# One field by 512 samples a chunk: the field groups folded into the top net's first layer, pooled sums kept in PSUM, 206 and 195 tiles fetched by SyncE and ScalarE

## The chip, the core and the metric

The kernel runs on one core of a Trainium2 chip. The metric is the time of one execution in microseconds of the device; of the kernel before there are three runs, with a median of 16514.44 us (16500.01 to 16524.78). The profile is of one further execution. Its engines are named as in its page: PE (TensorE matmul), PEld (its weight loads), DVE (VectorE), ACT (ScalarE), POOL (GpSimd), SP (SyncE).

## The reference

A click model for 16384 samples. Each sample has F = 69 indices and a label index into a table of 100001 rows of E = 96 floats. With u the rows of the indices and ql the row of the label:

```python
q = jnp.broadcast_to(ql[:, None, :], u.shape)
z = jnp.concatenate([q, u, q - u, q * u], axis=-1)
h = _dice(z @ W1 + b1, a1, EPS_DICE)           # 384 -> 64
h = h @ W2 + b2                                # 64 -> 16
att = h @ W3 + b3                              # 16 -> 1
pre = jnp.where(eff, u * att, 0.0)             # eff: index < 100000
pooled = jnp.einsum('gf,bfe->bge', window, pre).reshape(u.shape[0], G * E)
x = jnp.concatenate([pooled, ql], axis=-1)     # G = 10 groups of fields, and ql: 11 * 96
h = _dice(_bn_eval(x @ Wf1 + bf1, EPS_BN), af1, EPS_DICE)    # 1056 -> 200
h = _dice(_bn_eval(h @ Wf2 + bf2, EPS_BN), af2, EPS_DICE)    # 200 -> 80
return h @ Wf3 + bf3                           # 80 -> 1
```

`_dice(x, a)` is `(a * (1 - p) + p) * x` with p the sigmoid of x scaled. `window` is a 10 by 69 matrix of zeros and ones that says which fields a group sums. All is in float32.

## The kernel before, in words

The samples are worked in 32 blocks of 512. A block's 512 x 69 rows are cut into 69 chunks of 512 rows, and two chunks make a pair: 1104 pairs in all. 64 of a block's chunks hold 8 samples by 64 fields ("main"), the other five hold one of the last five fields for all 512 samples ("tail"). A chunk is four tiles of 128 rows.

*Fetching.* A tile is gathered by one indirect DMA on POOL (`gather`, L266). 369 of the 8832 tiles are fetched otherwise: 199 by SyncE and 170 by ScalarE, row by row with a DMA of 384 bytes each (`Singles.fetch`, L301) after loads of 32 offsets each into registers (L286). They land in `ring`, a separate buffer of 8 + 4 tiles, and PE waits for them by semaphore. SyncE starts a tile every 5.5 pairs. ScalarE issues 20 rows in every pair (`ACT_ROWS`), in its own program order between its activations. POOL also gathers 128 tiles of label rows. It writes `u`, of which `upool` has 15 buffers of a pair each.

*A pair.* The order is written out by hand: `at(step, work)` fills a plan, and the pair's step runs its pieces in the order given; each engine does its part of them in that order.

- `fetch` (L359): PE transposes the four tiles of each chunk (L325) into PSUM `ptr` (two buffers), DVE copies it to `uT` (L376) and multiplies it by the label's rows to `quT` (L379, L386).
- `hidden` (L388): PE makes `ph` of `uT` and `quT` (L399 to L403), both chunks side by side in 64 columns of the array each; ACT makes the sigmoid (L405) and a scale and shift of it (L406), DVE the product `y` (L407). The label's share of the first layer comes in through 32 further rows: a main chunk's `uT` has a one-hot pattern in them, and the weights `A` hold the label's products, made per block by `head_rows` (L342).
- Attention of main chunks: every fourth pair, `attend_rows` (L409) makes the products `prow` (L414), which ACT copies (L416); `spread` (L428) transposes them back (L431), and DVE multiplies with the window to `rw` (L436). `pool` (L448), seven pairs behind its fetch, multiplies the gathered tiles by `rw` on PE (16 rows of the profile per pair, `acc`, L325) and DVE copies the sums of the ten groups to `pooled` (L470). So a `u` buffer is held until its `pool`.
- Attention of tail chunks: `attend_tail` makes `pa` (L423) and DVE `pre = (pa + b) * uT` (L424).
- The top net of a block (`top1` to `top3`, L489 to L522), once per block, is spread over ten later pairs: 16 products a half (10 groups, the label, five tail fields) into `p` (L502), then activations, `p2` (L513) and `p3` (L521).

Near the end (`CLOSE` = 8 pairs) the order changes, and the last block's top net is done in four quarters of 128 samples.

PE writes a float32 matmul as two passes, which the profile counts singly (a transpose as one).

Of the kernel before, what the change touches and what calls it, by code (L numbers as in the profile page):

```python
# [11 lines left out]
F32 = mybir.dt.float32  # L12
# [15 lines left out]
FM = 64  # L28
NTAIL = F - FM
NS = BLK // FM  # L30
NMAIN = BLK // NS
NCH = NMAIN + NTAIL
NQ = BLK // P
NT = NCH * 4
NCOL = NT + NQ
NPAIR = NBLK * NCH // 2
# [4 lines left out]
POOL_LAG = 7  # L41

NIDS = 4

EARLY = 20

CLOSE = 8
# [15 lines left out]
def chunk_of(c):  # L63

    n, k = divmod(c, NCH)
    if n == NBLK - 1 and k >= EARLY:
        k = NMAIN + k - EARLY if k < EARLY + NTAIL else k - NTAIL
    return n, k


class Pack:
# [28 lines left out]
    wtile=(0, P, 2 * G),  # L100
)
FAR = Pack(
    wrow=(0, E, NTAIL * G),
    Wf1=(0, E, (G + 1) * D1),
# [6 lines left out]
    bf3=(0, P, 1),  # L111
)
# [3 lines left out]
def rec_kernel(  # L116
# [8 lines left out]
    far: bass.AP,  # L125
    out: bass.AP,
# [7 lines left out]
    upool = ctx.enter_context(tc.tile_pool(name="upool", bufs=15))  # L134
    tpool = ctx.enter_context(tc.tile_pool(name="tpool", bufs=4))
    ypool = ctx.enter_context(tc.tile_pool(name="ypool", bufs=6))
    rpool = ctx.enter_context(tc.tile_pool(name="rpool", bufs=2))
# [3 lines left out]
    def by_field(ap):  # L141

        return ap.rearrange("e (s o) -> e s o", o=1).to_broadcast([ap.shape[0], NS, FM])

# [19 lines left out]
    nc.sync.dma_start(out=wf, in_=far)  # L164

# [8 lines left out]
    Wp = w1[:, 3, :]  # L174


    As = [const.tile([P, NMAIN // 4, H1], F32, name=f"A{i}") for i in range(2)]
    nc.vector.tensor_sub(As[0][0:E, 0, :], w1[:, 1, :], w1[:, 2, :])
    nc.vector.tensor_copy(As[0][0:E, 1:, :], As[0][0:E, 0:1, :].to_broadcast([E, NMAIN // 4 - 1, H1]))
    nc.vector.tensor_copy(As[1][0:E], As[0][0:E])  # L180
    A = As[0][0:E, 0, :]
    uTs = [[const.tile([P, 512], F32, name=f"uT{v}_{i}") for i in range(3)] for v in range(4)]

    def ones():
        for i in range(3):
            for v in range(4):
                nc.vector.tensor_copy(
                    uTs[v][i][E:P, :].rearrange("e (s f) -> e s f", f=FM),
                    by_field(ident[E:P, E + v * NS : E + (v + 1) * NS]),
                )  # L190
# [17 lines left out]
    v2 = const.tile([P, 32], F32, name="v2")  # L208
    nc.vector.memset(v2, 0.0)
# [4 lines left out]
    R = NEAR.of(wn, "wtile")  # L214
    wr = FAR.of(wf, "wrow").rearrange("e (f g) -> e f g", g=G)


    wf1 = FAR.of(wf, "Wf1").rearrange("e (k n) -> e k n", n=D1)
# [20 lines left out]
    with tc.tile_pool(name="prep_ps", bufs=1, space=PSUM) as pps:  # L239
        pv = pps.tile([P, E], F32, name="pv")  # L240
        nc.tensor.matmul(pv, NEAR.of(wn, "W2T"), w3b, start=True, stop=True)
        nc.vector.tensor_copy(vrep, pv)
        for i in range(2):
            nc.vector.tensor_copy(v2[i * H1 : (i + 1) * H1, i : i + 1], pv[i * H1 : (i + 1) * H1, 0:1])
# [7 lines left out]
    ps_acc = ctx.enter_context(tc.tile_pool(name="ps_acc", bufs=1, space=PSUM))  # L252
    ps_m = ctx.enter_context(tc.tile_pool(name="ps_m", bufs=1, space=PSUM))


    V = const.tile([E, NTAIL, D1], F32, name="V")

    def tail_weights(f):
        nc.vector.tensor_scalar_mul(V[:, f, :], wf1[:, 0, :], wr[:, f, 0:1])
        for g in range(1, G):  # L260
            nc.vector.scalar_tensor_tensor(
                V[:, f, :], wf1[:, g, :], wr[:, f, g : g + 1], V[:, f, :], ALU.mult, ALU.add
            )

    def gather(table, dst, index):
# [5 lines left out]
        )  # L271

# [69 lines left out]
    def head_rows(n):  # L342

        for h in range(2):
            pc = ps_x.tile([P, NMAIN // 8, H1], F32, tag="x", name=f"pc{n}_{h}")
            for k in range(NMAIN // 8):
                x = (h * NMAIN // 8 + k) * 4 * NS
                nc.tensor.matmul(pc[E:P, k, :], qTs[n % 2][:, x : x + 4 * NS], Cq, start=True, stop=True)
            nc.scalar.copy(As[n % 2][E:P, h * NMAIN // 8 : (h + 1) * NMAIN // 8, :], pc[E:P])

    turns = [0] * 4

    def room(k):

        v = k % 4 if k < NMAIN else turns.index(min(turns))
        turns[v] += 1
        return uTs[v][turns[v] % len(uTs[v])]

    def fetch(i, between=None):  # L359

        u = upool.tile([P, 8, E], F32, tag="u", name=f"u{i}")
        uT = []
        quT = tpool.tile([E, 2, 512], F32, tag="quT", name=f"quT{i}")
        for j in range(2):
            if j == 1 and between:
                between()
            n, k = chunk_of(2 * i + j)
            ptr = ps_tr.tile([E, 512], F32, tag="tr", name=f"ptr{i}_{j}")
            for t in range(4):
                if single(2 * i + j, t):  # L370
                    wait_for_single(2 * i + j, t)
                else:
                    gather(rows, u[:, 4 * j + t, :], ids[n][:, 4 * k + t : 4 * k + t + 1])
                read_rows(nc.tensor.transpose, ptr[:, t * P : (t + 1) * P], u, 2 * i + j, t, ident)
            uT.append(room(k))
            nc.vector.tensor_copy(uT[j][0:E], ptr)  # L376
            q = qTs[n % 2][0:E]
            if k < NMAIN:
                nc.vector.tensor_tensor(  # L379
                    quT[:, j, :].rearrange("e (s f) -> e s f", f=FM),  # L380
                    ptr.rearrange("e (s f) -> e s f", f=FM),
                    by_field(q[:, k * NS : (k + 1) * NS]),
                    ALU.mult,
                )
            else:
                nc.vector.tensor_tensor(quT[:, j, :], ptr, q[:, 0:BLK], ALU.mult)  # L386
        return u, uT, quT

    def hidden(i, uT, quT):

        ph = ps_h.tile([P, 512], F32, tag="h", name=f"ph{i}")
        places = [chunk_of(2 * i + j) for j in range(2)]
        sums = [ph[j * H1 : (j + 1) * H1, :] for j in range(2)]
        for (n, k), p in zip(places, sums):
            if k >= NMAIN:
                nc.tensor.matmul(p, Cq, qTs[n % 2], start=True, stop=False)  # L396
        for j, ((n, k), p) in enumerate(zip(places, sums)):
            if k < NMAIN:
                nc.tensor.matmul(p, As[n % 2][:, k // 4, :], uT[j], start=True, stop=False)  # L399
            else:  # L400
                nc.tensor.matmul(p, A, uT[j][0:E], start=False, stop=False)  # L401
        for j, p in enumerate(sums):
            nc.tensor.matmul(p, Wp, quT[:, j, :], start=False, stop=True)  # L403
        y = ypool.tile([P, 512], F32, tag="y", name=f"y{i}")
# [349 lines left out]
```

## Time and profile before

| | |
|---|---|
| runs | 16514.44, 16500.01, 16524.78 us |
| the profiled execution: span from its first to its last instruction | 10780.4 us |
| its mean granted TensorE clock | 0.749 |
| what lies around the span, to the median of the runs | 5734.0 us, of which the trace shows nothing |
| instructions | 204439 |
| moved by DMA | 460.70 MB, 43 GB/s on average |
| gathers on POOL | 8463 + 128 |
| rows issued by SyncE, ScalarE | 25472, 21760 |
| pairs of chunks | 1104 |

For the profiled execution there is no time beside its span; the runs in the first row were made without a profile.

How to read the page: in its list of groups, a line gives the source line, the engine, the operation, what is written and read, the count, the busy time in us with the mean of one in ns, and the idle time of the engine before it with what ended most of it. In a timeline, each row is the start in us, the duration in us, the engine and what it does, with the number of instructions merged; an engine's name with a q is its sequencer, which issues DMAs and waits. In a view of one source line, each row has the least, median and largest duration in ns and the first and last start. In the waits, a row gives who waited for whom, the total in us, how often, and the longest.

### The profile page before, as it was taken

Reading aid. Unit: us, or ns where it says so; the run is one execution under the profiler, and the core shown is the slowest. Engines: PE = TensorE matmul, PEld = TensorE weight load, DVE = VectorE, ACT = ScalarE, POOL = GpSimd, SP = SyncE. Lnnn points to the kernel's source line nnn. Section 1 sums busy time; section 2 is a strip of 40 time slices with the busy share of each in tenths; the row PEclk is TensorE's granted clock in tenths of the full one; section 3 lists DMA queues with packets and bytes.
Section 4 is the critical chain, followed back from the end, with each engine's and each line's share of the span. In section 5 each row is a group of like instructions: output and inputs, shape, how many; then the busy total and the mean of one; then the engine's idle time right before and its main releaser. Section 6 shows DMA issues by size and latency. Waiting matters only on the chain.

```text
span 10780.4 us, 204439 instructions
## 1 busy us (share of the span) xinstructions
PE 8756.9 (81%) x41797; PEld 4310.8 (40%) x41797; DVE 4235.1 (39%) x7535; ACT 1884.4 (17%) x2761; POOL 8110.8 (75%) x8597
## 2 busy tenths in 40 slices
PE   6888888888887788877888788888887887888888
PEld 3434444434433344433433344333343343443335
DVE  4333333333333333333333343333333334333333
ACT  1111111111111111111111111111111111111112
POOL 7777777777777777777777777777777777777776
PEclk7777777677777777777777777777777777777778
DMA  2222222222222222222222222222222222222221
GB/s 50 42 42 42 45 42 42 42 42 45 42 42 42 45 42 42 42 42 45 42 42 42 42 44 42 42 42 42 44 42 42 42 42 44 42 42 42 42 42 34
DMA packets 372495, 460.70 MB, mean 43 GB/s; under 512 B 232114, under 2 KB 232626, under 8 KB 371106
## 3 DMA queue, kind: packets, MB, share of 16 engines
q0 software_dynamic: 274912, 422.81, 18.9%
q1 hardware_dynamic: 52802, 16.36, 1.0%
q10 hardware_dynamic: 43520, 8.44, 0.7%
q14 instruction: 925, 7.58, 0.2%
q8 instruction: 336, 5.51, 0.2%
HBM read 446.81 MB, written 0.07 MB: 41 GB/s over the span
## 4 chain that ended last, share of the span: by engine, by line
POOL 40%; PE 21%; issue 19%; DMA 12%; ACTq 6%; ACT 2%; DVE 1%; POOLq 0%
POOL u L266 40%; DMA u<-in_rows,ids 12%; ACTq L301 4%; PE acc L325 4%; PE p L502 4%; PE ph L399 3%; PE ph L403 3%; PE ptr L325 2%; PE prow L414 1%; ACTq L286 1%; PE pa L423 1%; ACT y L405 1%; POOL q L266 1%; PE ph L396 1%; PE ph L401 1%
## 5 line engine op out<-in xcount | busy, mean ns | idle before, releaser
L266 POOL DMA_INDIRECT u<-in_rows,ids x8463 | 7989.1, 944 | 2583.5 <-issue 2389.6
L325 PE MATMUL ptr<-ident,u 128*96 128x128 f32 x8463 | 1925.1, 332 | 1606.1 <-DMA u<-in_rows,ids 1555.6
L407 DVE TENSOR_TENSOR y<-ph,y 128x512 f32<-128x512 f32 x1104 | 763.5, 692 | 4972.6 <-ACT y L406 4699.0
L325 PEld LDWEIGHTS acc<-rw,u 128*96 128x96 f32 x15702 | 1674.4, 188 | 1332.5 <-issue 840.4
L325 PEld LDWEIGHTS ptr<-ident,u 128*96 128x96 f32 x8463 | 1131.6, 151 | 2282.7 <-DMA u<-in_rows,ids 1853.2
L325 PE MATMUL acc<-rw,u 128*96 128x20 f32 x15702 | 1792.0, 259 | 212.0 <-DVE rw L436 177.6
L376 DVE COPY uT<-ptr 96x512 f32<-96x512 f32 x2208 | 1489.0, 674 | 739.9 <-PE ptr L325 737.5
L405 ACT ACTIVATE y<-ph 128x512 f32<-128x512 f32 x1104 | 658.8, 597 | 6119.1 <-PE ph L403 3304.1
L399 PE MATMUL ph<-uT,A 128*64 128x512 f32 x4096 | 1598.9, 856 | 0.0
L403 PE MATMUL ph<-quT,wn 96*64 96x512 f32 x4416 | 1540.5, 767 | 0.0
L379 DVE TENSOR_TENSOR quT<-ptr,qT 96x512 f32<-96x512 f32 x2048 | 1379.1, 673 | 0.0
L406 ACT ACTIVATE y<-y,wn,na1c 128x512 f32<-128x512 f32 x1104 | 897.9, 813 | 36.6
L403 PEld LDWEIGHTS ph<-quT,wn 96*64 96x64 f32 x4416 | 429.4, 183 | 1002.5 <-issue 1001.8
L502 PE MATMUL p<-pooled,wf 96*100 96x512 f32 (+1 forms) x1400 | 667.7, 624 | 0.0
L414 PE MATMUL prow<-y,v 128*32 128x512 f32 x2208 | 507.2, 885 | 65.4 <-DVE y L407 57.6
L399 PEld LDWEIGHTS ph<-uT,A 128*64 128x64 f32 x4096 | 259.6, 172 | 609.6 <-issue 605.5
L416 ACT COPY row<-prow 128x512 f32<-128x512 f32 (+1 forms) x277 | 161.6, 583 | 1733.2 <-issue 675.0
L470 DVE COPY pooled<-acc 96x160 f32<-96x160 f32 x1008 | 420.5, 417 | 99.1 <-PE acc L325 97.6
L502 PE MATMUL p<-pre,V 96*100 96x512 f32 (+1 forms) x700 | 398.0, 714 | 11.1 <-DVE x L485 10.8
L502 PEld LDWEIGHTS p<-pooled,wf 96*100 96x100 f32 x1400 | 249.6, 190 | 316.5 <-issue 316.5
L436 DVE SCALAR_TENSOR_TENSOR rw<-patt,bb,wn 128x320 f32<-128x320 f32 x554 | 276.1, 539 | 116.8 <-PE patt L431 114.7
L485 DVE SCALAR_TENSOR_TENSOR x<-p,wf,g 100x512 f32<-100x512 f32 (+3 forms) x105 | 73.9, 704 | 523.6 <-ACT g L484 523.5
(72 smaller groups left out, 2706.1 us busy)
## 6 DMA issues: line engine op xcount, KB each, us to landing
ring<-in_rows SPq DMA_DIRECT2D x25472, 0.4 KB
ring<-in_rows ACTq DMA_DIRECT2D x21760, 0.4 KB
u<-in_rows,ids POOLq DMA_INDIRECT x8463
ids<-in_idx SPq DMA_DIRECT2D x8, 560.0 KB, 3.9
q<-in_emb,ids POOLq DMA_INDIRECT x128
wf<-in_far SPq DMA_DIRECT2D x1, 1209.0 KB, 8.3
wn<-in_near SPq DMA_DIRECT2D x1, 236.0 KB, 3.4
offsets<-in_single_rows SPq DMA_DIRECT2D x1, 192.0 KB, 2.5
```

The source lines that it names most:

```text
L266: nc.gpsimd.indirect_dma_start(out=dst, out_offset=None, in_=table, in_offset=bass.IndirectOffsetOnAxis(ap=index, axis=0),)
L301: d = self.engine.dma_start(out=ring[r : r + 1, b], in_=row_bytes[:, bass.ds(self.values[r], ROW_BYTES)]).then_inc(self.sems[k], 16)
L325: ins = op(out, ring[:, at[0]].bitcast(F32) if at else u[:, 4 * (c % 2) + t, :], other, **how)
L376: nc.vector.tensor_copy(uT[j][0:E], ptr)
L379: nc.vector.tensor_tensor(quT[:, j, :].rearrange("e (s f) -> e s f", f=FM), ptr.rearrange("e (s f) -> e s f", f=FM), by_field(q[:, k * NS ...
L399: nc.tensor.matmul(p, As[n % 2][:, k // 4, :], uT[j], start=True, stop=False)
L403: nc.tensor.matmul(p, Wp, quT[:, j, :], start=False, stop=True)
L405: nc.scalar.activation(y, ph, AF.Sigmoid, scale=S_DICE)
L406: nc.scalar.activation(y, y, AF.Identity, bias=a1c, scale=na1c)
L407: nc.vector.tensor_mul(y, ph, y)
L414: nc.tensor.matmul(pr[32 * k : 32 * (k + 1), :], v2, ys[b + k], start=True, stop=True)
L502: nc.tensor.matmul(p1, w[:, h * DH : (h + 1) * DH], x, start=(k == 0), stop=(k == KTOP - 1))
```

## The change

Every chunk is now one field by 512 samples, as the tail chunks were. `pool`, `attend_rows`, `spread` and the main chunks' one-hot rows go.

- The window is folded into the top net's first layer: for each field f, `V[:, f]` (96 x 200) is the sum of the `Wf1` blocks of the groups that hold f. `field_weights` makes it at the start: 32 groups of up to seven matmuls, each group copied from PSUM by DVE or ACT in turn.
- For every chunk, `attend` makes `pa` on PE and `pre` on DVE, and `top1` adds `V` times `pre` into two banks of PSUM (100 outputs each) that stay open for the 69 chunks of a block.
- The label's share of the first layer now is copied into rows 96 to 127 of `uT` and `quT` (`cT`, `label_rows`, by ACT, 14 copies a block); `hidden` multiplies all 128 rows by `AW` and `BW`.
- ACT's part of a pair is cut up: the sigmoid, four rows, the scale and shift, then the other 19 rows in threes with further jobs between them (`busy`).
- SyncE fetches 206 tiles, one every 5.3 pairs; ScalarE 195 tiles at 23 rows a pair, with 8 ring buffers in place of 4. `upool` has 6 buffers in place of 15, which a pair's transposes set free.

The diff, cut to its core:

```diff
-SP_CHUNKS = [2 * (int(5.5 * s) + 6) + 1 for s in range(199)]
+SP_STEPS = 5.3
+SP_AHEAD = 8
+SP_CHUNKS = [2 * (int(SP_STEPS * s) + SP_AHEAD) + 1 for s in range(206)]
 SP_RING = 8
-ACT_ROWS = 20
-ACT_CHUNKS = [2 * ((s + 1) * P // ACT_ROWS + 2) for s in range(170)]
-ACT_RING = 4
+ACT_ROWS = 23
+ACT_FIRST = 4
+ACT_GROUP = 3
+ACT_AHEAD = 5
+ACT_CHUNKS = [2 * ((s + 1) * P // ACT_ROWS + ACT_AHEAD) for s in range(195)]
+ACT_RING = 8
...
 def chunk_of(c):
-    n, k = divmod(c, NCH)
...
+    return divmod(c, F)
...
-    upool = ctx.enter_context(tc.tile_pool(name="upool", bufs=15))
+    upool = ctx.enter_context(tc.tile_pool(name="upool", bufs=6))
...
+    V = const.tile([E, F, D1], F32, name="V")
...
+    def field_weights(k):
+        x, q = divmod(k, NV)
+        x0, x1 = x * PER_BANK, min((x + 1) * PER_BANK, D1 // NV)
+        pv = ps_x.tile([E, PER_BANK, F], F32, tag="x", name=f"pV{k}")[:, 0 : x1 - x0, :]
+        at = slice(32 * q, 32 * q + G)
+        for x in range(x0, x1):
+            nc.tensor.matmul(pv[:, x - x0, :], wg[at, x, :], window[at], start=True, stop=True)
+        copy = nc.scalar.copy if k % 2 else nc.vector.tensor_copy
+        n = q * (D1 // NV)
+        copy(V[:, :, n + x0 : n + x1], pv.rearrange("e n f -> e f n"))
...
+    def hidden(i):
+        ph = ps_h.tile([P, BLK], F32, tag="h", name=f"ph{i}")
+        sums = [(2 * i + j, ph[j * H1 : (j + 1) * H1, :]) for j in range(2)]
+        for c, p in sums:
+            nc.tensor.matmul(p, AW, uTs[c % NUT], start=True, stop=False)
+        for c, p in sums:
+            nc.tensor.matmul(p, BW, quTs[c % NQUT], start=False, stop=True)
+        y = ypool.tile([P, BLK], F32, tag="y", name=f"y{i}")
         nc.scalar.activation(y, ph, AF.Sigmoid, scale=S_DICE)
...
+    def gate(i):
+        nc.scalar.activation(ys[i], ys[i], AF.Identity, bias=a1c, scale=na1c)
+        nc.vector.tensor_mul(ys[i], phs.pop(i), ys[i])
...
+    def attend(c):
+        i, j = divmod(c, 2)
+        pa = ps_x.tile([E, BLK], F32, tag="x", name=f"pa{c}")
+        at = slice(j * H1, (j + 1) * H1)
+        nc.tensor.matmul(pa, vrep[at], ys[i][at], start=True, stop=True)
+        pres[c] = ppool.tile([E, BLK], F32, tag="pre", name=f"pre{c}")
+        nc.vector.scalar_tensor_tensor(pres[c], pa, bb[0:E], uTs[c % NUT][0:E], ALU.add, ALU.mult)
...
+    def top1(c):
+        n, k = chunk_of(c)
+        if k == 0:
+            p1s[n] = [ps_p.tile([DH, BLK], F32, tag=f"p{h}", name=f"p1_{n}_{h}") for h in range(2)]
+            for h, p in enumerate(p1s[n]):
+                nc.tensor.matmul(p, wq[:, h * DH : (h + 1) * DH], qTs[n % 2][0:E], start=True, stop=False)
+        pre = pres.pop(c)
+        for h, p in enumerate(p1s[n]):
+            nc.tensor.matmul(p, V[:, k, h * DH : (h + 1) * DH], pre, start=False, stop=(k == F - 1))
...
+    def busy(i):
...
+        rows = [(r, min(r + ACT_GROUP, ACT_ROWS)) for r in range(ACT_FIRST if i >= 2 else 0, ACT_ROWS, ACT_GROUP)]
+        while rows or jobs:
+            if rows and i < c:
+                scalar_rows(i, *rows.pop(0))
+            else:
+                rows = []
+            if jobs:
+                jobs.pop(0)()
...
     for i in range(c):
...
+        if i >= 2:
+            at(i, call(hidden, i - 2), call(scalar_rows, i, 0, ACT_FIRST))
         if i >= 3:
...
+            at(i, call(attend, 2 * i - 6), call(attend, 2 * i - 5))
         if i >= 2:
...
+            at(i, call(gate, i - 2))
+        if i >= 4:
+            due = late + [2 * i - 8, 2 * i - 7]
+            late = [due.pop()] if due[-1] % F == 0 else []
+            tops(i, due)
+        at(i, call(busy, i), call(fetch, i))
...
+    for k in range(NV * ((D1 // NV + PER_BANK - 1) // PER_BANK)):
+        at(k // 8, call(field_weights, k))
```

`tops` puts a `top1` for each chunk given, and after a block's last one the activations of its top net (`top1_gates`, `top2`, `top3`) into the jobs of the next steps. The last pairs (`CLOSE` = 6) run `hidden` and `gate` between a pair's two fetches and end with the last block's top net in one piece of 512 samples. With that, ACT gets 3 rows more a pair and no longer the copies of `prow` and of `A`; PE gets two `pa` and four top matmuls a pair and loses 16 passes of `acc`.

More of the change, by code (lines that the diff above doesn't have):

```diff
@@ L387, in fetch @@
[L387 to L404, printed above, removed]
-        nc.scalar.activation(y, ph, AF.Sigmoid, scale=S_DICE)
-        nc.scalar.activation(y, y, AF.Identity, bias=a1c, scale=na1c)
-        nc.vector.tensor_mul(y, ph, y)
-        return y
@@ new lines, in rec_kernel, with finish @@
+    for i in range(c + 2, NPAIR):
+        tops(i, both(i - 3))
+        at(i, call(attends, i - 2), call(fetch, i, call(hide, i - 1)))
+    i = NPAIR
+    tops(i, both(i - 3))
+    at(i, call(hide, last), call(attends, i - 2))
+    tops(i, both(i - 2))
+    at(i, call(store, 0, (NBLK - 1) * NQ), call(attends, last))
+    tops(i, both(last))
+    def finish():
+        n = NBLK - 1
+        for job in top1_gates(n):
+            job()
+        for job in top2(n):
+            job()
+        top3_last(n)
```

428 lines of the change are left out of this document (147 added, 281 removed).

## Prediction

> **What bounds the kernel now.** I read the page's busy shares first, then the source view of the gather line, then the waits, then the timeline of single engines. The page's head, its clock row and the source view of L266:
>
> ```profile
> span 10780.4 us, 204439 instructions
> PE 8756.9 (81%) x41797; PEld 4310.8 (40%) x41797; DVE 4235.1 (39%) x7535; ACT 1884.4 (17%) x2761; POOL 8110.8 (75%) x8597
> PEclk7777777677777777777777777777777777777778
> ...
> L266 POOL DMA_INDIRECT u<-in_rows,ids x8463: 940/944/1093, 8.3 to 10734.6; - x197
> L266 POOL DMA_INDIRECT q<-in_emb,ids x128: 940/944/1097, 3.2 to 10272.5; - x128
> ```
>
> PE looks busiest, but the matmul ends are modelled. POOL shows 75%, and that is full: the waits view has its idle time in pieces of at most 0.3 us, one behind nearly every gather.
>
> ```profile
> POOL u L266 <- issue: 2389.6, 7828, 0.3
> POOL u L266 <- DMA u<-in_rows,ids: 79.4, 260, 0.3
> ```
>
> The last column is the longest wait. A gather takes 0.944 us and 0.30 us pass before the next, whatever the rest of the core does. POOL issues 8463 + 128 = 8591 gathers from 3.2 to 10734.6 us: 10731.4 / 8590 = 1.2493 us each, without a hole. The program is one POOL queue with 10780.4 - 10734.6 = 45.8 us of work behind its last gather. A pair of chunks has 10731.4 / 1104 = 9.72 us.
>
> The median of the runs is 16514.44 us, which is 5734.0 us more than this span. No row says where that time lies. Either it lies outside the span and a saving counts once, or an unprofiled run is longer throughout (16514.44 / 10780.4 = 1.532) and a saving counts 1.532 times. I make the sum in the span's time and carry both readings.
>
> **The change, part by part.**
>
> *Gathers.* SyncE and ScalarE fetch 206 + 195 = 401 tiles in place of 199 + 170 = 369. POOL has 8832 - 401 + 128 = 8559 gathers, 32 fewer: 32 x 1.2493 = **-40.0 us**. A pair then has 8559 x 1.2493 / 1104 = 9.685 us. Every other engine has to stay under this, since POOL may run only six pairs ahead (`upool` has 6 buffers).
>
> *PE.* Pooling by 16 narrow passes per pair goes, with `prow` and `patt`; two `pa` and four top-net matmuls per pair come. The timeline of PE at both of its speeds:
>
> ```profile
> 5053.52 1.98 PE L396 MATMUL ph<-qT,Cq 97*64 97x512 f32 x4
> 5055.28 1.92 PE L401 MATMUL ph<-uT,A 96*64 96x512 f32 x4
> 5056.99 1.92 PE L403 MATMUL ph<-quT,wn 96*64 96x512 f32 x4
> 5058.84 2.75 PE L325 MATMUL acc<-rw,u 128*96 128x20 f32 x16
> 5061.42 1.92 PE L325 MATMUL ptr<-ident,u 128*96 128x128 f32 x8
> 5063.27 2.03 PE L423 MATMUL pa<-y,vrep 64*96 64x512 f32 x4
> ...
> 5073.33 1.10 PE L423 MATMUL pa<-y,vrep 64*96 64x512 f32 x2
> 5074.35 1.08 PE L399 MATMUL ph<-uT,A 128*64 128x512 f32 x4
> 5075.26 1.03 PE L403 MATMUL ph<-quT,wn 96*64 96x512 f32 x4
> 5076.22 1.53 PE L325 MATMUL acc<-rw,u 128*96 128x20 f32 x16
> ...
> 5208.54 3.60 PE L502 MATMUL p<-pooled,wf 96*100 96x512 f32 x8
> 5211.97 0.60 PE L431 MATMUL patt<-ident,row 128*128 128x128 f32 x4
> ```
>
> One matmul is two rows, and start to start is what counts. At full clock `ph` takes 0.91 + 0.96 = 1.87 us, `pa` 1.02 us, four top matmuls 3.43 us and eight transposes about 0.97 us (half of their cold 1.85 us, and a little). The sum is **7.3 us** a pair. At half clock it is 3.56 + 1.95 + 6.86 + 1.85 = **14.2 us** (the top matmuls taken twice as long). POOL's 9.685 us lies between. Which clock PE gets, the same rows show: after dense work at half clock it goes to full (from 5069 us on), and the clock row stands at 7 because PE, ahead of POOL, waits for gathers and falls back. With 7.3 of 9.685 us filled and a backlog as soon as it is slow, PE corrects itself, and I take it as hidden.
> [...]
>
> *DVE.* Per pair two `pre` operations of 0.74 us come and the copies of `acc` and the `rw` products go, 2.7 + 0.7 + 1.5 = 4.9 of 9.685 us. Hidden by the gathers.
>
> ```profile
> L376 DVE COPY uT<-ptr 96x512 f32<-96x512 f32 x2208 | 1489.0, 674 | 739.9 <-PE ptr L325 737.5
> L407 DVE TENSOR_TENSOR y<-ph,y 128x512 f32<-128x512 f32 x1104 | 763.5, 692 | 4972.6 <-ACT y L406 4699.0
> L424 DVE SCALAR_TENSOR_TENSOR pre<-pa,bb,uT x160: 729/740/749, 356.2 to 10570.6; 96x512 f32<-96x512 f32 x160
> ```
>
> *ScalarE's queue.* It issues 23 rows a pair in place of 20, its table loads with them, and four of them now stand between the two activations. ACT's timeline, a pair without and one with a load of 32 offsets, and the loads:
>
> ```profile
> 5004.08 9.05 ACTq L301 DMA_DIRECT2D ring<-in_rows  x20
> ...
> 5015.05 0.60 ACT L405 ACTIVATE y<-ph 128x512 f32<-128x512 f32 x1 [1.30 <-PE ph L403]
> 5015.68 0.81 ACT L406 ACTIVATE y<-y,wn,na1c 128x512 f32<-128x512 f32 x1
> 5015.75 6.37 ACTq L301 DMA_DIRECT2D ring<-in_rows  x20
> ...
> L286 ACTq TENSOR_LOAD <-offsets x680: 2105/2274/2522, 16.3 to 10592.8; - x170
> ```
>
> A row is 6.37 / 20 = 0.3185 us, a load adds 9.05 - 6.37 = 2.68 us. Before: 20 x 0.3185 + 20/32 x 2.68 + 0.7 (the queue stands from 5015.05 to 5015.75 while the second activation waits for the first) = 8.75 of 9.72 us. After: 23 x 0.3185 + 23/32 x 2.68 = 9.25 us, and 0.1 to 0.7 us for the activations, as four rows fill the wait or not: 9.35 to 9.95 us against 9.685. I take 9.4 us, since four rows (1.27 us) are longer than that wait. **0 us**, with 0.28 us to spare; the upper end would add 0.265 x 1104 = 293 us. What queues behind a late row is the next sigmoid, behind it DVE's product and PE's `pa`.
>
> *SyncE's queue.* 128 rows for every 5.3 pairs in place of 5.5.
>
> ```profile
> L301 SPq DMA_DIRECT2D ring<-in_rows x25472: 227/228/482, 6.7 to 10349.8; - x199
> ...
> SPq L301 <- PE ptr L325: 84.8, 36, 13.2
> SPq L301 <- PE acc L325: 27.5, 7, 10.9
> ```
>
> (10349.8 - 6.7 - 84.8 - 27.5) / 25471 x 128 = 51.4 us a tile, its loads included, its waits for a free ring buffer not. The budget is 5.3 x 9.685 = 51.3 us. SyncE falls behind by 0.1 us a tile, 21 us over 206; its first tile, due in pair 8 (some 90 us in), is issued by 60 us. So it arrives in time, just: **0 us**, or up to +40 if its rows cost 0.5% more beside ScalarE's 3200 further ones.
>
> *Start and end.* 32 groups of seven matmuls build `V` in the first four steps. By the nearest rows, 16 passes of `acc` in 1.53 us warm or 2.75 us cold, their 448 passes are 43 to 77 us of PE. Six buffers of gathers (58 us) cover that; what is not covered is at most 19 us. At the end, the chain of waits behind the last gather holds these pieces of the last block's top net:
>
> ```profile
> 10752.33 3.56 PE p L502 x32
> ...
> 10758.31 2.79 PE p L502 x24
> ...
> 10766.23 7.80 PE p L502 x56
> ```
>
> These 14.2 us go; three groups of four top matmuls (3.43 us each, 10.3 warm and 20.6 cold) and two `pa` with their `pre` come. I keep 45.8 us, with -14 to +20. **0 us.**
>
> The sum: 10780.4 - 40.0 = 10740 us of span. For the run that is 16514.44 - 40.0 = 16474 or, if stretched, 16514.44 - 61.3 = 16453. Nothing prefers one; I take the middle, **16464 us**, -0.31%. About 0.2% (33 us) is what can be told from no change.
>
> PE's and ACT's steady state, which these terms rest on. PE, one pair before (`acc` is pooling; the top net's `p` stands in some pairs only):
>
> ```order
> L399 MATMUL ph_84199<-uT_1_106,A_98 64x512
> L399 MATMUL ph_84199<-uT_1_109,A_98 64x512
> L403 MATMUL ph_84199<-quT_84039,wn 64x512 x2
> L325 MATMUL acc_84293<-rw_83996,u_83095 96x20 x8
> L325 MATMUL ptr_0_84305<-ident,u_84303 96x128 x4
> L325 MATMUL ptr_1_84316<-ident,u_84303 96x128 x4
> ```
>
> and one pair after:
>
> ```order
> L376 MATMUL ph_90889<-uT_104,AW 64x512
> L376 MATMUL ph_90889<-uT_105,AW 64x512
> L378 MATMUL ph_90889<-quT_116,BW 64x512
> L378 MATMUL ph_90889<-quT_117,BW 64x512
> L393 MATMUL pa_90900<-y_90762,vrep 96x512
> L393 MATMUL pa_90904<-y_90762,vrep 96x512
> L406 MATMUL p_13_0_86087<-pre_90770,V 100x512
> L406 MATMUL p_13_1_86088<-pre_90770,V 100x512
> L406 MATMUL p_13_0_86087<-pre_90774,V 100x512
> L406 MATMUL p_13_1_86088<-pre_90774,V 100x512
> L317 MATMUL ptr_90999<-ident,u_90998 96x128 x3
> ```
>
> The transposes, which free POOL's buffers, now stand behind six wide matmuls more. ACT, two pairs before:
>
> ```order
> L405 ACTIVATE y_47695<-ph_47690 128x512
> L406 ACTIVATE y_47695<-y_47695,wn,na1c 128x512
> L301 DMA ring<-in_rows 1x384 x20
> L405 ACTIVATE y_48146<-ph_48141 128x512
> L406 ACTIVATE y_48146<-y_48146,wn,na1c 128x512
> ```
>
> and after:
>
> ```order
> L380 ACTIVATE y_35268<-ph_35263 128x512
> L293 DMA ring<-in_rows 1x384 x4
> L385 ACTIVATE y_35268<-y_35268,wn,na1c 128x512
> L293 DMA ring<-in_rows 1x384 x19
> L380 ACTIVATE y_35723<-ph_35718 128x512
> ```
>
> Four rows moved between the activations, and `row` and `A` copies are gone from this queue.
>
> **The rivals.** *ScalarE's queue sets the pace (slower).* For it: 9.4 of 9.685 us is 97% full, one load more or less shifts a pair by 2.68 us, and each sigmoid waits for PE, whose pair varies from 7.3 to 14.2 us. Against it: an early or late pair evens out over `ph`'s two buffers and the ring's eight. It decides once the queue needs over 9.685 us with its waits. At 9.8 us (0.4 us of waits a pair not made up) it costs 0.115 x 1104 = 127 us, net +87: 16601, stretched 16648. [...]
>
> *SyncE comes late (same).* The 20 to 40 us above eat the 40 saved: 16514.
>
> *PE sets the pace (slower).* If the clock stays at the 0.75 of before, half the time at each speed, a pair takes 2 / (1/7.3 + 1/14.2) = 9.64 us and with a block's extra matmuls (5 us in 34.5 pairs) 9.8: +127, net +87, as above. Against it stands that a backlog raises the clock.
>
> *The fewer gathers don't count (same).* If the 5734 us hide another bound, 40 us of POOL vanish: 16514.
>
> **How the numbers follow.** Forecast 0.56, ScalarE 0.22, SyncE 0.12, PE 0.05, no effect 0.05. Of the forecast 0.03 ends within 0.2%. Faster 0.53, same 0.03 + 0.12 + 0.05 = 0.20, slower 0.27. The low end is 16453 less 14 x 1.532 for a shorter end, 16432; the high end 16640 takes in ScalarE's case nearly to its stretched value. The forecast's own range is 16432 to 16500.
>
> **What would show it.** Right: gathers of 8559 at 1.249 us with no wait over 0.3 us, a span near 10740, a mean clock above 0.85, a last gather near 10695 us. ScalarE's case: POOL waits of many us for `ptr`, and ACT's rows without idle between them. SyncE's: PE waiting at `ring` transposes late in the run. PE's: the clock row still at 7. The prediction is wrong if POOL's pace changes at all.

## The result, and the profile after

| kernel | median us | range | runs |
|---|---|---|---|
| before | 16519.61 | 16500.01 to 16531.76 | 4 |
| after | 16819.26 | 16800.13 to 16838.16 | 4 |

The change is slower: 1.018 times before, with a 95% interval of 1.0165 to 1.0194 (+299.65 us), a small loss but clear of the noise. The forecast was 16464 us with a range up to 16640: the kernel became slower where faster was forecast, and it lies above the range. The profiled execution of after took 16800.13 us with a span of 16798.4 us: here nothing lies around the span. The page's head, its clock row, and the chain that ended last, by engine:

```profile
span 16798.4 us, 194662 instructions
PE 10259.2 (61%) x32079; PEld 3761.9 (22%) x32079; DVE 5103.7 (30%) x7995; ACT 1981.7 (12%) x2866; POOL 8076.6 (48%) x8565
PEclk8877777777777777777777777777787777777778
...
SPq 64%; issue 35%; PE 1%; ACTq 0%; DMA 0%; ACT 0%; DVE 0%; another core or an unknown queue 0%; DVEq 0%
```

POOL showed 75% in the trace before, which was full; here it shows 48%, and the chain is SyncE's sequencer and its issue time almost alone. The waits view names who waits for whom (total us, times, longest):

```profile
POOL u L255 <- PE ptr L317: 5373.5, 564, 29.5
PEld ptr L317 <- DMA ring<-in_rows: 3048.6, 178, 32.3
```

POOL now stands 5373.5 us for PE's transposes, which free its buffers, and PE stands 178 times before a tile of single rows (there are 401), up to 32.3 us at a time. The source view of the line that issues the rows has one row for each queue:

```profile
L293 SPq DMA_DIRECT2D ring<-in_rows x26368: 1/228/1502, 7.4 to 16684.7; - x200
L293 ACTq DMA_DIRECT2D ring<-in_rows x24960: 1/213/1408, 22.8 to 16538.8; - x200
...
SPq L293 <- PE ptr L317: 0.5, 2, 0.3
```

(The last line is from the waits: SyncE hardly waits for a free ring buffer.) SyncE issues rows from 7.4 to 16684.7 us, nearly the whole span: 16677.3 / 26367 x 128 = 81.0 us a tile of 128 rows, where the prediction had 51.4. The median issue is the old 228 ns, but the longest is 1502 ns in place of 482, and even the MOVE ahead of a row does not always take its 29 ns, as the next place shows. POOL's and PE's timelines around 4650 us, in after:

```profile
4645.34 0.94 POOL L255 DMA_INDIRECT u<-in_rows,ids  x1 [0.30 <-issue]
4646.59 0.94 POOL L255 DMA_INDIRECT u<-in_rows,ids  x1 [0.31 <-issue]
4671.21 0.94 POOL L255 DMA_INDIRECT u<-in_rows,ids  x1 [23.68 <-PE ptr L317]
...
4661.73 0.45 PE L317 MATMUL ptr<-ident,ring 128*96 128x128 f32 x1 [25.23 <-DMA ring<-in_rows]
```

and SyncE's rows there, by the source view cut to two windows, 4630 to 4648 us while POOL gathers without a pause, and 4651 to 4671 us while POOL stands:

```profile
L293 SPq DMA_DIRECT2D ring<-in_rows x18: 4/228/1399, 4629.8 to 4646.1; - x18
L293 SPq MOVE ring<-in_rows x18: 3/29/711, 4630.1 to 4647.5; - x18
...
L293 SPq MOVE ring<-in_rows x54: 29/29/29, 4651.0 to 4670.8; - x54
L293 SPq DMA_DIRECT2D ring<-in_rows x54: 227/228/280, 4651.0 to 4670.9; - x54
```

While POOL gathers, SyncE gets about one row a us out (18 in 4630.1 to 4647.5), with MOVEs of up to 711 ns. While POOL stands, it is 54 rows in 19.9 us, 2.7 a us. These windows hold no loads of offsets; over the whole trace, loads included and POOL taken as standing where its next gather comes over 3 us late, the rates are 1.2 and 2.3 rows a us. So the rows are late, PE waits for the tile of rows, POOL runs its six pairs ahead and stands, SyncE catches up, and the cycle begins again.

In the trace of before, the same view cut to 5000 to 5018 us, with POOL gathering all the time:

```profile
L301 SPq DMA_DIRECT2D ring<-in_rows x46: 227/228/262, 5000.7 to 5017.9; - x46
```

There SyncE has 2.7 rows a us beside the gathers. That execution was unlike the timed runs, and that is the 5734.0 us which no row explained. The chips differ here: on one of them before takes 10784.82 us (below). On which chip the first trace was taken is not on record; its span fits that one.

### The profile page after: what moved, and what is told of

The parts are those of the page before. It is cut to its first block, busy times and chain, and to the rows that moved or that the text cites. A ratio compares the mean times of both kernels' runs of the same rounds, so it can differ in the third digit from the quotient of the medians.

```text
span 16798.4 us, 194662 instructions
## 1 busy us (share of the span) xinstructions
PE 10259.2 (61%) x32079; PEld 3761.9 (22%) x32079; DVE 5103.7 (30%) x7995; ACT 1981.7 (12%) x2866; POOL 8076.6 (48%) x8565
## 3 DMA queue, kind: packets, MB, share of 16 engines
q0 software_dynamic: 273888, 421.24, 11.9%
q1 hardware_dynamic: 54738, 18.20, 0.5%
## 4 chain that ended last, share of the span: by engine, by line
SPq 64%; issue 35%; PE 1%; ACTq 0%; DMA 0%; ACT 0%; DVE 0%; another core or an unknown queue 0%; DVEq 0%
SPq L293 54%; SPq L278 10%; PE p L406 0%; ACTq L293 0%; PE ph L376 0%; PE ph L378 0%; PE ptr L317 0%; PE pa L393 0%; DMA ring<-in_rows 0%; ACTq L278 0%; PE p L428 0%; SPq L145 0%; DMA offsets<-in_single_rows 0%; PE pq L331 0%
## 5 line engine op out<-in xcount | busy, mean ns | idle before, releaser
L255 POOL DMA_INDIRECT u<-in_rows,ids x8431 | 7955.0, 944 | 8610.6 <-PE ptr L317 5373.5
L406 PE MATMUL p<-pre,V 96*100 96x512 f32 x8832 | 4768.9, 690 | 2.3 <-DVE pre L395 2.3
L393 PE MATMUL pa<-y,vrep 64*96 64x512 f32 x4416 | 1641.7, 806 | 2694.2 <-issue 2043.5
L406 PEld LDWEIGHTS p<-pre,V 96*100 96x100 f32 x8832 | 1609.1, 193 | 3337.8 <-issue 3333.8
L395 DVE SCALAR_TENSOR_TENSOR pre<-pa,bb,uT 96x512 f32<-96x512 f32 x2208 | 1548.6, 739 | 2244.1 <-PE pa L393 936.6
L376 PE MATMUL ph<-uT,AW 128*64 128x512 f32 x4416 | 1539.4, 723 | 470.0 <-issue 235.7
L378 PE MATMUL ph<-quT,BW 128*64 128x512 f32 x4416 | 1483.8, 691 | 71.3 <-issue 63.0
L393 PEld LDWEIGHTS pa<-y,vrep 64*96 64x96 f32 x4416 | 354.3, 197 | 3842.9 <-issue 3036.2
L317 PE MATMUL ptr<-ident,u 128*96 128x128 f32 x8431 | 1137.7, 273 | 25.5 <-remote 10.6
L378 PEld LDWEIGHTS ph<-quT,BW 128*64 128x64 f32 x4416 | 388.7, 158 | 879.4 <-issue 853.7
L376 PEld LDWEIGHTS ph<-uT,AW 128*64 128x64 f32 x4416 | 263.8, 151 | 811.5 <-issue 525.3
```

Source lines behind the costliest of these rows:

```text
L255: nc.gpsimd.indirect_dma_start(out=dst, out_offset=None, in_=table, in_offset=bass.IndirectOffsetOnAxis(ap=index, axis=0),)
L317: ins = op(out, ring[:, at[0]].bitcast(F32) if at else u[:, 4 * (c % 2) + t, :], other, **how)
L376: nc.tensor.matmul(p, AW, uTs[c % NUT], start=True, stop=False)
L378: nc.tensor.matmul(p, BW, quTs[c % NQUT], start=False, stop=True)
L393: nc.tensor.matmul(pa, vrep[at], ys[i][at], start=True, stop=True)
L395: nc.vector.scalar_tensor_tensor(pres[c], pa, bb[0:E], uTs[c % NUT][0:E], ALU.add, ALU.mult)
```

## The experiments

Ratios are to the kernel before, run beside it on the same chip. The runs came to four chips: three where before takes 16.5 or 16.8 ms, as in the timed runs (A chips below; one of them was met twice), and one where it takes 10784.82 us, as in the first trace (the B chip). The B chip was met at one time only, so what is put down to it could also be of that time. A ratio of one chip is compared with those of its kind.

### On an A chip (before 16825.56 us): what is the bound?

*before_again*, the kernel before, unchanged, for a trace of a run like the timed ones.

> The kernel before, unchanged, for a second trace. Theory A (the row issues of SyncE and ScalarE stall, and SyncE's queue sets the pace of both kernels): a span near 16500 us as in the runs, not the 10780 of the first trace; SyncE needs about 82 us for a tile of 128 rows instead of 51.4, in steps of 0.7 us. Theory B (only the changed kernel is bound by something new, its loop over PE, ACT and DVE with six buffers): a span of 10780 us again with SyncE at 51.4 us a tile.

Measured: 0.9994 (0.9984 to 1.0005). Its head, its chain and its rows:

```profile
span 16817.9 us, 204439 instructions
...
SPq 62%; issue 36%; PE 1%; ACTq 0%; DMA 0%; ACT 0%; DVE 0%; POOL 0%
...
L301 SPq DMA_DIRECT2D ring<-in_rows x25472: 1/228/1469, 6.7 to 16698.9; - x199
```

16692.2 / 25471 x 128 = 83.9 us a tile. In the runs, before too was bound by SyncE's rows and not by POOL.

*no_rows*, all 401 tiles back to POOL's gathers.

```diff
-SP_CHUNKS = [... for s in range(206)]
+SP_CHUNKS = [... for s in range(0)]
-ACT_CHUNKS = [... for s in range(195)]
+ACT_CHUNKS = [... for s in range(0)]
```

> The changed kernel with no tile fetched by SyncE and ScalarE: POOL gathers all 8832 tiles and the 128 of labels. Theory A: with the row issues gone POOL sets the pace, 8960 x 1.2493 = 11194 us and some 45 at the end: a span of 11200 to 11300, a third less than the changed kernel. Theory B: the loop keeps its pace, 15.2 us a pair, and the span stays within 3% of 16800.

Measured: 13205.26 us, 0.7845 (0.7829 to 0.7860). Without a single row on SyncE or ScalarE the changed kernel beats both kernels by over a fifth. It does not come down to POOL's 11200 us, though:

```profile
span 13212.3 us, 90601 instructions
...
PE 59%; another core or an unknown queue 27%; DVE 6%; issue 6%; ACT 2%; DMA 0%; DVEq 0%; POOL 0%
...
ACT y L380 <- remote: 5802.6, 446, 31.4
```

PE makes most of the chain, and 27% is time until a release that the trace does not name (`remote` in the waits). That miss says that rows are not all that is held up on this chip; no_rows_u14_b comes back to it.

*sp_only*, ScalarE's 195 tiles to POOL, SyncE's 206 kept.

```diff
-ACT_CHUNKS = [... for s in range(195)]
+ACT_CHUNKS = [... for s in range(0)]
```

> The changed kernel with SyncE's 206 tiles and none of ScalarE's. Theory A, with the stalls a matter of each queue alone: SyncE still needs 81 us a tile and the span stays at 16700 to 16800. Theory A, with the stalls made by the two queues together: SyncE falls back to about 51.4 us a tile and POOL sets the pace with 8754 gathers, 10940 us and 45. Theory B: within 3% of 16800.

Measured: 16759.81 us, 0.9960 (0.9943 to 0.9978), SyncE at 80.7 us a tile. SyncE is as slow without ScalarE's rows; the two queues do not slow each other into this.

*old_counts*, the changed kernel with the tiles of before.

```diff
-SP_STEPS = 5.3
+SP_STEPS = 5.5
-SP_CHUNKS = [... for s in range(206)]
+SP_CHUNKS = [... for s in range(199)]
-ACT_ROWS = 23
+ACT_ROWS = 20
-ACT_CHUNKS = [... for s in range(195)]
+ACT_CHUNKS = [... for s in range(170)]
```

> The changed kernel with the tile counts of before: 199 by SyncE every 5.5 pairs, 170 by ScalarE at 20 rows a pair. Theory A: SyncE's 199 tiles at 81 us are 16120 us and the ends, 16250, so below the kernel before or equal to it (ratio 0.98 to 1.00). Theory B: the loop keeps its pace, ratio 1.015 to 1.02 as with the new counts.

Measured: 1.0081 (1.0061 to 1.0101), 84.7 us a tile. Equal counts take away more than half of the loss, not all of it: the expectation was a little too low, and the rest of the change (the new loop, with its six buffers of `u`) costs 0.8%.

### On a second A chip (before 16486.23 us): what slows SyncE?

*after_again*, the changed kernel, unchanged.

> The changed kernel once more, unchanged, beside the kernel before on the same chip. Theory B (SyncE's queue of single rows sets the pace, at some 81 us a tile of 128 rows, because its steps are slow while POOL's gathers run): SyncE again at 80 to 83 us a tile, the span within 1% of 206 tiles of that, and the ratio to before between 1.010 and 1.022. Theory C (the ratio of 1.018 belonged to the chip or the day): within 0.998 to 1.005.

Measured: 1.0187 (1.0157 to 1.0216). The loss is there again, so it is no accident of one set of runs.

*act_only*, SyncE's tiles to POOL, ScalarE's 195 kept (`range(206)` becomes `range(0)`).

> The changed kernel with ScalarE's 195 tiles alone; SyncE's 206 go to POOL's gathers (same output). Theory B: ScalarE issues some 23 rows per pair at about the price of SyncE's, 0.63 us a row, so 24960 rows take 15700 us and ScalarE's queue takes SyncE's place as the bound: 15300 to 16300 us. Rival D (only SyncE's queue is hindered; ScalarE's rows are as cheap as in the first trace, 0.3185 us): no queue is a bound, and the time is that of the kernel without any rows, 13000 to 13600 us.

Measured: 14715.22 us, 0.8909 (0.8873 to 0.8945), between the two theories. ScalarE's queue is then 51% of the chain, so its rows are hindered as well (against D), but at a lower price than B gave: (14715.22 - 13138.15) / 195 = 8 us for each of its tiles over the time that the kernel without rows took on this chip (no_rows_u14_b, below; it has 14 buffers of `u`).

*before_no_rows*, the kernel before with `range(0)` in both lists.

> The kernel before with its 199 and 170 single-row tiles gathered by POOL like the others (same output). Theory B: the rows are what costs in both kernels; without them the time falls to the next bound. By POOL alone, 8960 gathers of 1.2493 us are 11194 us; the new loop without rows took 13205 us. If the old loop is the better one without rows, 11200 to 12800 us; if the new loop is the better one, 13500 to 14500 us. Rival (rows are no bound in the old loop, which is late for another reason): 16000 us or more.

Measured: 13329.21 us, 0.8088 (0.8074 to 0.8101), between the two ranges given. The old loop, too, gains a fifth by giving up its single rows.

*quarter_gathers*: one tile of each chunk is gathered; the chunk's other transposes read it again. All rows of SyncE and ScalarE stay.

```diff
-                else:
+                elif t == 0:
                     gather(rows, u[:, 4 * j + t, :], ids[n][:, 4 * k + t : 4 * k + t + 1])
...
-        ins = op(out, ring[:, at[0]].bitcast(F32) if at else u[:, 4 * (c % 2) + t, :], other, **how)
+        ins = op(out, ring[:, at[0]].bitcast(F32) if at else u[:, 4 * (c % 2), :], other, **how)
```

> The changed kernel with only the first of each chunk's four tiles gathered; the other transposes read that tile again (so three quarters of the fetched rows are left out, and the output is another). SyncE's and ScalarE's rows stay as they are. Theory B (SyncE's steps are slow because POOL's gathers run): with some 2200 gathers instead of 8559 SyncE needs 50 to 60 us a tile, and the time is 10500 to 12800 us. Rival E (SyncE's steps are slow whatever POOL does): SyncE still at 78 to 84 us a tile, 16300 us or more.

Measured: 10970.73 us, 0.6658 (0.6645 to 0.6672). The span, SyncE's rows, and what PE still waits for:

```profile
span 10966.9 us, 188439 instructions
...
L293 SPq DMA_DIRECT2D ring<-in_rows x26368: 2/228/829, 7.4 to 10859.5; - x200
...
PE ptr L317 <- DMA ring<-in_rows: 642.0, 109, 12.7
```

The same 26368 rows beside the same ScalarE rows take 10852.1 / 26367 x 128 = 52.7 us a tile, close to the 51.4 of the first trace. So on an A chip it is POOL's gathers that slow SyncE's steps. Rival E is out. The run does not tell the issue of a gather from its transfers: both fell to about a quarter (2208 + 128 = 2336 gathers in place of 8559, and 74752 packets on POOL's queue in place of 273888).

### On the B chip (before 10784.82 us)

*before_206*, the kernel before with 206 tiles on SyncE and no other edit.

```diff
-SP_CHUNKS = [2 * (int(5.5 * s) + 6) + 1 for s in range(199)]
+SP_CHUNKS = [2 * (int(5.3 * s) + 6) + 1 for s in range(206)]
```

> The kernel before with the changed kernel's 206 tiles on SyncE, one every 5.3 pairs, and nothing else of the change (same output). Theory B with a rate: SyncE issues about 1.0 row a us while POOL gathers and 2.5 rows a us while POOL stands, so seven more tiles cost 7 x 128 / 2.5 = 358 us of standing POOL and save 7 x 1.25 = 9 us: a ratio of 1.021 to before (1.017 to 1.025). Rival F (the new loop makes the 1.8%, not the count): 0.997 to 1.004.

*after_199*, the changed kernel with `SP_STEPS = 5.5` and `range(199)`; ScalarE keeps its 195 tiles.

> The changed kernel with 199 tiles on SyncE, one every 5.5 pairs, as before; ScalarE keeps its 195. Theory B: the seven tiles are the whole loss, so the ratio falls from 1.0187 to 0.998 (0.993 to 1.003). Rival F: it stays at 1.015 to 1.020.

*no_rows_u14*, no_rows with `upool` at 14 buffers in place of 6.

> The changed kernel without any single rows (all 401 tiles gathered by POOL, same output) and with 14 buffers of u in place of 6. If POOL's waits for PE there come of too little lead, it goes to 11800 to 12900 us (POOL alone: 8960 x 1.2493 = 11194). If the rest of the loop sets the pace, it stays within 1% of the 0.7845 of the run with 6 buffers.

*sp_60*, the changed kernel with 60 tiles on SyncE (`SP_STEPS = 18.2`) and none on ScalarE.

> The changed kernel with 60 tiles on SyncE, one every 18.2 pairs, and none on ScalarE (same output). Theory B: 7680 rows are fewer than SyncE can issue beside the gathers (about one a us), so SyncE is no bound, and the time is that of the kernel without rows or a little less, 0.775 to 0.79 of before. Rival G (each single row costs a fixed time wherever it lies; 206 tiles cost 3550 us more than none): 60 tiles cost 1030 us, 0.84 to 0.85.

None of these expectations was written for the chip that they met. All 15 runs of before took 10781.64 to 10791.28 us there, the first trace's 10780.4 us again. The measured ratios are 0.9995 (0.9985 to 1.0004) for before_206, 1.0353 (1.0338 to 1.0367) for after_199, 1.0412 (1.0396 to 1.0428) for no_rows_u14 and 1.0343 (1.0327 to 1.0359) for sp_60. On this chip POOL's queue is the bound, as the prediction read it. The span of no_rows_u14, and its gathers:

```profile
span 11228.3 us, 90593 instructions
PEclk9999999999999999999999999999999999999999
...
L255 POOL DMA_INDIRECT u<-in_rows,ids x8832: 940/945/962, 8.3 to 11193.8; - x197
```

8832 + 128 gathers by 1.2493 us are 11194 us; it took 11229.9, which leaves about 36 us for the ends. For sp_60, with the same 36 us, the sum is 8900 x 1.2493 + 36 = 11155 us; it took 11155.78. And before_206 is 6.2 us shorter with its seven fewer gathers (8.7 by the sum).

after_199 breaks that rule: 8566 x 1.2493 + 36 = 10738 us, and it took 11165.96. Its chain, its two queues of rows on the page (packets, MB, share of 16 engines' span), and POOL's wait for transfers:

```profile
DMA 32%; POOL 20%; PE 17%; ACTq 16%; issue 13%; ACT 1%; DVE 0%; POOLq 0%; DVEq 0%
...
q1 hardware_dynamic: 52946, 17.86, 2.7%
q10 hardware_dynamic: 49920, 9.68, 2.2%
...
POOL u L255 <- DMA u<-in_rows,ids: 547.8, 893, 3.1
```

beside those of before_206:

```profile
q1 hardware_dynamic: 54594, 16.70, 1.1%
q10 hardware_dynamic: 43520, 8.44, 0.8%
...
POOL u L266 <- DMA u<-in_rows,ids: 85.2, 279, 0.3
```

SyncE's packets took 0.027 x 16 x 11169.5 / 52946 = 91 ns each in place of 0.011 x 16 x 10769.0 / 54594 = 35 ns, and by the trace's packets a gather's last one ended 3.26 us after its start (median) where it is 2.17 us in before_206. ScalarE's queue is 16% of the chain. So on the B chip the changed loop loses 428 us with SyncE's 199 and ScalarE's 195 tiles, and nothing with 60 tiles on SyncE alone. The old loop loses nothing there with nearly as many rows (48128 in before_206, 50432 in after_199). What is left is ScalarE's 23 rows a pair or the order of the new loop; no run tells these two apart.

### On the second A chip again (before 16483.5 us), and on a third (before 16768.82 us)

*before_206_b*, before_206 once more.

> The kernel before with 206 tiles on SyncE, one every 5.3 pairs, again. If before takes some 16500 us on this chip: theory B (SyncE's rows pace it; seven more tiles cost 7 x 128 / 2.5 us less 9 us of gathers) 1.017 to 1.025 of before, rival F (the new loop makes the loss) 0.997 to 1.004. If before takes some 10785 us: 0.999 to 1.000, as the first time.

Measured: 16793.73 us, 1.0188 (1.0174 to 1.0202). The chain:

```profile
SPq 63%; issue 36%; PE 1%; DMA 0%; another core or an unknown queue 0%; DVE 0%; ACT 0%
```

Seven more tiles on SyncE (one every 5.3 pairs for one every 5.5), and not one other edit, cost the kernel before 310 us, as much as the whole change.

*after_act170*, the changed kernel with ScalarE's 170 tiles at 20 rows a pair.

> The changed kernel with ScalarE's part as before (170 tiles, 20 rows a pair) and SyncE's 206. If before takes some 16500 us on this chip: ScalarE's rows are no bound there, 1.012 to 1.022 of before. If before takes some 10785 us: theory H (ScalarE's 23 rows a pair make the gathers late) 8584 gathers x 1.2493 + 36 = 10760 us, 0.996 to 1.001, with gathers landing in 2.2 us; rival I (the new loop itself makes them late) 1.02 to 1.035.

Measured: 16957.56 us, 1.0284 (1.0268 to 1.0300), above the range given. With equal counts the new loop is 16957.56 / 16793.73 = 1.0098 of before_206_b, which agrees with the 1.0081 of old_counts; and the 25 further tiles of ScalarE bring 1% back, from 1.0284 to the 1.0187 of after_again (same chip, another time).

*no_rows_u14_b*, no_rows_u14 once more.

> The changed kernel without single rows and with 14 buffers of u. If before takes some 16500 us on this chip: with 6 buffers it was 0.7845 of before and POOL waited 398 us for PE and 1408 us for a release that the trace does not name; if that was too little lead, 0.70 to 0.765, else 0.775 to 0.79. If before takes some 10785 us: 1.041, as the first time.

Measured: 13138.15 us, 0.7968 (0.7956 to 0.7981), just above the range for the case in which more buffers do not help: 13205.26 us with 6. What holds the loop at 13.1 to 13.3 ms on A chips, 2 ms above POOL's 11.2, is not POOL's lead. On the same chip before_no_rows took 13329.21 us, so without rows the new loop is 1.4% the faster one.

The trace shows in part what does hold it. The waits of ACT and DVE for PE, in no_rows_u14_b (A) and then in no_rows_u14 (B), the same program:

```profile
ACT y L380 <- remote: 6014.4, 483, 30.9
DVE pre L395 <- remote: 3050.7, 383, 19.7
...
ACT y L380 <- PE ph L378: 8854.5, 1103, 16.4
DVE pre L395 <- PE pa L393: 2202.0, 1101, 5.8
```

`remote` means here that the semaphore update which ended the wait came when no instruction that raises this semaphore had just ended. Over all engines such waits come to 12449 us in no_rows_u14_b and to nothing in no_rows_u14. A case of it in no_rows:

```profile
6006.10 0.61 PE L317 MATMUL ptr<-ident,u 128*96 128x128 f32 x4 [1.68 <-issue]
6009.70 0.69 DVE L368 COPY uT<-ptr 96x512 f32<-96x512 f32 x1 [3.70 <-remote]
```

By the trace, PE's four transposes had ended at 6006.72 us. The updates of PE's semaphore stand at 6008.23, 6008.96 and 6009.68 us, some 0.72 us apart, and DVE starts at the last. Of all recorded updates of that semaphore, 59% come more than 0.2 us after the last end of a matmul that raises it in no_rows_u14_b, none in no_rows_u14, and 0.8% in quarter_gathers, on an A chip with a quarter of the gathers. (The traces of A chips miss some of these updates: 10651 of 13515 are there.) So on A chips dense gathers hold up PE's signals to the other engines too, and not only the rows.

*sp_60_b*, sp_60 once more, and *sp_130*, with 130 tiles on SyncE.

```diff
-SP_STEPS = 5.3
+SP_STEPS = 8.4
-SP_CHUNKS = [... for s in range(206)]
+SP_CHUNKS = [... for s in range(130)]
-ACT_CHUNKS = [... for s in range(195)]
+ACT_CHUNKS = [... for s in range(0)]
```

> The changed kernel with 60 tiles on SyncE, one every 18.2 pairs, none on ScalarE. If before takes some 16500 us on this chip: theory B (rows cost only where they are more than SyncE can issue beside the gathers) 0.775 to 0.805 of before, as without rows; rival G (a fixed 17 us a tile) 0.84 to 0.86. If before takes some 10785 us: 1.034, as the first time.

> The changed kernel with 130 tiles on SyncE, one every 8.4 pairs, none on ScalarE. If before takes some 16500 us on this chip: theory B with its rate, 1.0 row a us for the 11030 us of 8830 gathers and 2.5 a us besides, asks 13270 us for 16640 rows, just above the 13140 without rows: 0.79 to 0.82 of before; rival G 15350 us, 0.93. If before takes some 10785 us: 8830 gathers x 1.2493 + 36 = 11067 us, 1.026.

Measured: 13204.56 us, 0.7875 (0.7862 to 0.7888) for 60 tiles, 13380.13 us, 0.7989 (0.7968 to 0.8010) for 130. Sixty tiles are free (13205.26 us without any, on another A chip), 130 just begin to show; a fixed price for each row (rival G) is out. The chain of sp_60_b still has PE at its head; that of sp_130 has SyncE there, and PE behind it:

```profile
SPq 35%; issue 28%; PE 21%; another core or an unknown queue 12%; DVE 3%; ACT 1%; POOL 0%; DMA 0%; DVEq 0%; POOLq 0%
```

*sp_only_b*, sp_only once more.

> The changed kernel with SyncE's 206 tiles and none on ScalarE, again. If before takes some 16500 us on this chip: 0.993 to 1.000 as the first time, so ScalarE's 195 tiles cost 2% there; 1.01 to 1.02 if that was the other chip. If before takes some 10785 us: 8754 gathers x 1.2493 + 36 = 10973 us, 1.017, with gathers landing in 2.2 us if ScalarE's rows made them late; 1.03 or more with gathers in 3.2 us if the new loop does.

Measured: 16667.71 us, 0.9945 (0.9927 to 0.9963), as the first time. From 130 to 206 tiles, on one chip, each tile costs (16667.71 - 13380.13) / 76 = 43 us.

## Why the prediction was wrong

*The step that failed is the first, the bound.* With it failed the zero for SyncE's queue, which was taken to deliver a tile in 51.4 us. "The program is one POOL queue" was read from one execution with a span of 10780.4 us, while the runs took 16514.44. The prediction saw the gap and carried it as a constant or a factor. The runs showed a third thing, another bound: SyncE's rows at 81 to 84 us a tile. On the B chip the reading of that trace is exact to some us, but the runs to be forecast were not made on such a chip.

*The sign follows from it.* Where SyncE is the bound, a tile that moves from POOL to SyncE is no saving of 1.25 us but a cost. SyncE gets 1.0 row a us out while POOL gathers and some 2.7 while it stands, so a further tile needs about 128 / 2.7 = 47 us of standing POOL. Seven tiles: some 330 us by this estimate (390 with the whole trace's 2.3 rows a us), and 310 measured with before_206_b.

*Of the rivals,* "SyncE comes late" had the place right (PE waits at the `ring` transposes) and the price wrong: 51.4 us a tile came from the same trace, so the most that it could cost was 40 us. "The fewer gathers don't count", because the gap hides another bound, was the right thought with 5%; it stopped at no effect and did not ask whether the hidden bound could be a queue to which the change adds work. The signs that the prediction named for its rivals came all at once: POOL waits for `ptr`, PE waits at `ring`, and the clock row stands mostly at 7. The chain tells which of them is the cause.

*The other terms.* The 1.8% on an A chip is 1.9% for SyncE's seven tiles, 0.8 to 1.0% for the rest of the change, and 1% back with ScalarE's 25 further tiles. The forecast had zero for that rest and a gain of 40 us for all 32 tiles together. PE and DVE at zero, and the clock above 0.85, held where POOL is the bound: sp_60's mean clock was 0.937, and it fits POOL's sum within 1 us. The ends did as well: 34.5 us behind the last gather in no_rows_u14, where the forecast had 45.8 us less up to 14. ScalarE's term is in doubt there: it was zero, at most 293 us, in the forecast, and after_199 lost 428 us, with 16% of its chain on ScalarE's queue and 32% on transfers, gathers almost alone (12% in before_206). The changed kernel itself was not run on the B chip. With seven tiles fewer it lost 3.5% there, and seven tiles made no difference to the kernel before, so the forecast gain would most likely have failed there too, by another step.

*What stays open.* Why gathers hold up the other engines on the A chips and not on the B chip was not settled: the traces show that it is so, and the program is the same. The fetching of instructions does not explain it as far as its records go: its packets of 8 KB took 425 ns on average in after and 427 ns in the first trace of before. Nor was it settled why ScalarE's 25 further tiles gain 160 us on an A chip, of which POOL's gathers are 31 us, while taking all of its tiles away gains more (0.9960 and 0.9945 of before, against 1.0187); nor whether the late gathers on the B chip come of the 23 rows a pair or of their places in the new loop, since after_act170 and sp_only_b met A chips.

The best of the kernels run depends on the chip. Where before takes 16.5 or 16.8 ms, the changed kernel with no single rows or few is the fastest that computes the whole output (0.7845; 0.7968 with 14 buffers and 0.7875 with 60 tiles on SyncE, on other chips). Where it takes 10.8 ms, before with 206 tiles cannot be told from before, and none of the changed kernels run there reaches it.

## What to carry to other kernels

Compare the trace's span with the timed runs before reading anything else in it: when they differ by half, the bound in the trace need not be the bound of the runs, and every price in it is in doubt. Here the gap was a queue that is slower in the runs; ask of each queue to which the change adds work what happens if its price is half as high again. Work that is moved to an idle queue is free only up to what that queue can do beside the others: on the A chips here that was somewhere from 60 to 130 tiles, and 206 cost 43 us for each tile above 130.

## What the runs showed of the hardware

On A chips the sequencers of SyncE and ScalarE are slowed while POOL's indirect gathers follow each other. SyncE gets about one row a us out in place of 2.7, with single steps of 0.7 or 1.4 us that take 0.03 or 0.23 us otherwise. ScalarE, in after, issues 16 rows from 4631.5 to 4646.8 us, while POOL gathers (with MOVEs of up to 1402 ns), and 38 rows from 4650.7 to 4670.9 us, while POOL stands (every MOVE 29 ns). It takes dense gathers: with a quarter of them a tile of SyncE's took 52.7 us in place of 81.0. PE's signals come late there as well, in the case above some 0.72 us apart, and the waits put down to `remote` are 12449 us in no_rows_u14_b, 5 us in quarter_gathers, and none in any trace of the B chip. The transfers themselves are no slower in after: a gather's last packet ends 2.15 us after the gather's start (median), where the first trace of before has 2.17 us, and SyncE's 54738 packets took 26 ns on average, where 52802 took 34 ns there. The queues of POOL and SyncE in after (packets, MB, share of 16 engines' span):

```profile
q0 software_dynamic: 273888, 421.24, 11.9%
q1 hardware_dynamic: 54738, 18.20, 0.5%
```

POOL's queue moved 273888 / 8559 = 32 packets a gather, half of them of 4 bytes; ScalarE's queue moved one packet of 4 bytes for each of its 24960 rows. What it is in a gather that holds up SyncE, ScalarE and PE's signals was not shown.

For one program the chips differed more than any edit of this study: before took 10785 us on the B chip, and 16483 to 16520 and 16769 to 16826 us in the other sets of runs.
